# Graph attention and graph convolution, two layers: hub steps one y block later, and the pair with block 0 ninth of ten

## The chip, the cores and the metric

The kernel runs on one core of a Trainium2 chip. The core has five engines with instruction queues of their own: TensorE (PE in the profile; its weight loads are PEld), VectorE (DVE), ScalarE (ACT), GpSimd (POOL) and SyncE (SP), which here only issues transfers. The metric is device time in microseconds, the median of several runs.

## The reference

There are 2708 rows (nodes) of 1024 features, all float32, and a 0/1 adjacency matrix `adj` of 2708 x 2708 with few ones a row; early rows have more than late ones.

```python
# layer 0
q, k, v = x @ W_q.T + b_q, x @ W_k.T + b_k, x @ W_v.T + b_v
z = (q @ k.T) / sqrt(1024) * adj
z = where(z == 0, -10000, z)
x = layernorm(x + relu(softmax(z, axis=1) @ v))
# layer 1
x = layernorm(x + adj @ (x @ weight) + bias)
```

Because the masked scores vanish in the softmax, only the scores on a row's own neighbours matter. A row without neighbours gets the mean over all rows.

## The kernel before, in words

The kernel does not form the 2708 x 2708 score matrix. It finds each row's neighbour list, gathers the neighbours' rows of `x` by indirect transfers, and works on those. `(x @ W_q.T) @ (x @ W_k.T).T` is rewritten as `y @ x.T` with `y = x @ M`, where `M` is the product of the two weight matrices; `adj @ (x @ W)` is computed as `(adj @ x) @ W`. If a list is longer than the kernel has room for, a flag is raised and a dense version runs instead; with these inputs it does not.

**Blocks.** The rows are sorted by number of neighbours in two families and cut into 22 blocks of up to 128 rows. `SLOTS` says how many neighbour slots a block has: 15, 11, 8, 6, 5, 4, 3, 2 for blocks 0 to 7, then 13, 5, 4, 4, 3, 3, 3, 2, 2, 2, 1, 1, 0, 0. A gather of one slot is one POOL instruction: one row of 4 KB for each of 128 partitions. The 32 rows with the most neighbours are the *hub*. Their neighbours are dealt out in shares of 11 slots over 128 partitions (`tab_h`, `valid_h`, `part`); block 0 with 15 slots holds the rest of its rows and shares. When block 0 is transposed for the matmuls ("flipped"), `flip_shares` (L840 to L852) adds the hub's shares `part` and block 0's `r` together with one-hot matrices `to_h` and `to_0`. So block 0's flip needs both the hub's sums and block 0's own.

**Stages.** First come the weights' product `M` (L709) and the neighbour lists (`list_columns`, L235 to L245, on DVE). Then there is the loop over the first family's y blocks, `for b in range(FAMILY)`, b from 0 to 7. In it, `y_block(b)` issues 16 matmuls (L378; two records each in the profile), evicts each half on DVE (L320), has SP load a later block of `x` (L297) and stores y (L369). `row_constants` (L746) makes one dot product a row on DVE. `sort_begin(1)` and `sort_end(1)` sort the second family; `sort_end` has two matmuls, L632 and L634. `next(deal)` runs one step of the hub's dealing, the generator `deal_hub`. Its steps are:

- step zero, POOL gathers of the hub rows' adjacency;
- step one, a search for the up to 80 neighbours in each quarter row on DVE (L503 and L505), the count `n_q` (L508), and a store of the keys (POOL, L514);
- step two, matmul L519 of `n_q` over the four quarters and the sizes of the shares on DVE (L521 to L528);
- step three, matmuls L531 and L532, DVE work on places and positions (L534 to L567, with `to_h` last), and a POOL gather of the hub's records;
- step four, transpose L570 and the masks `far_h` and `far_0`;
- step five, eleven small POOL gathers (`found`, L435);
- step six, the tables `valid_h`, `tab_h` and `less_h`.

Steps five and six are issued in the next loop, at the second family's first and fifth block. L519, L531/L532 and the sort's L632 all write the tile `mm`, of which there is one buffer.

Then the second family's y blocks run with attention among them: an attention job gathers y (`yg`, L435), which needs the stores of the first eight y blocks, and the neighbours' x (`g`, L441, nine buffers), scores them (L917) and sums (L974, L1058). Then pairs of blocks are projected with `W_v`, normalised and scattered to `x1`.

**Layer 1** (L1290 to L1390) works the blocks in ten pairs, `units`, which are numbered from 0 here. For each `units[i]`, `sum_rows` gathers and sums the neighbours' rows of `x1` (POOL L441, DVE L1307 and L1310), `turn1` flips the two sums (PE L836, or L849 for block 0) and makes sums and differences of their halves (DVE L1097 to L1100), `gather_x1` brings the residual `xr` (ScalarE L1320 copies the bias, and a POOL gather at L435 adds the rows to it), and `work1` does seven products of half matrices in place of eight (`pair_products`, matmuls at L306; evictions at L320 and L1347). `finish1` normalises and scatters to `out` (POOL L823). In iteration i the order is: finish `units[i-1]`, flip `units[i+1]` and gather its residuals, gather and sum `units[i+3]`, then the products of `units[i]`. The blocks 20 and 21, which have no neighbours, are finished behind `units[4]` and `units[6]`.

**Order.** A planner fixes the order of every engine's queue when the kernel is built. It goes by priority, which is the order in which the code issues instructions (evictions are marked more urgent), and by when it believes inputs to be ready. On the chip each queue runs in that order, and an instruction whose input is late holds up what is behind it.

Of the kernel before, what the change touches and what calls it, by code (L numbers as in the profile page):

```python
# [80 lines left out]
def sparse_part(ctx, tc, x, xT, adj, wqT, wkT, wvT, bq, bk, bv, w1, b1, out):  # L81
# [29 lines left out]
    with es:  # L111
# [69 lines left out]
        def bcast_rows(dst, col):  # L181

            for g in range(DC // 4):
                tr = p_tr.tile([P, 4, P], F32, name="tr")
                for k in range(4):
                    c = g * 4 + k
                    nc.tensor.transpose(tr[:, k, :], col[:, c:c + 1].to_broadcast([P, P]), ident)
                nc.scalar.copy(dst[:, g * HALF:(g + 1) * HALF], tr.rearrange("p a b -> p (a b)"))
# [37 lines left out]
        def list_columns():  # L226
            b = listed[0]
            listed[0] += 1
            n, a = rows[b], loaded[b]

            nc.scalar.activation(junk[:n], a[:n], AF.Sign, accum_out=cnt[:n, b:b + 1])  # L231
            nc.scalar.activation(junk[:n], a[:n], AF.Relu, scale=-1.0, accum_out=neg[:n, b:b + 1])
            at = lists.tile([P, RANGES, 8], U16, name="at_a", bufs=2)
            for i in range(RANGES):
                nc.vector.max_index(at[:n, i], ones[:n, :8], a[:n, cuts[i] + 8 * i:cuts[i + 1] + 8 * i + 8])  # L235
            there = lists.tile([P, RANGES, 8], F32, name="there", bufs=2)
            nc.vector.tensor_tensor(there[:n], at[:n], ends[:n], op=ALU.is_lt)
            few = lists.tile([P, 8 * RANGES], F32, name="few", bufs=2)
            few3 = few.rearrange("p (i k) -> p i k", k=8)
            nc.vector.tensor_tensor(few3[:n], at[:n], base[:n], op=ALU.add)  # L240
            nc.vector.tensor_tensor(few3[:n], few3[:n], there[:n], op=ALU.mult)
            for i in range(0, KEYS, 8):
                nc.vector.max(keys[:n, b, i:i + 8], few[:n])
                if i + 8 < KEYS:
                    nc.vector.match_replace(few[:n], keys[:n, b, i:i + 8], few[:n], 0.0)  # L245
            load_adj()
# [115 lines left out]
        def load_last():  # L362
            r0, n = (NB - 1) * P, rows[-1]
            nc.sync.dma_start(out=x_last[:, :, :n], in_=xT[:, r0:r0 + n].rearrange("(c p) n -> p c n", p=P))
# [6 lines left out]
        def y_block(b):  # L371
            yo = yos[b % 3]
            to, base = halves_of(yo), halves_of(y_bc)
            firsts = []
            for h in range(NH):
                po = bank()
                for c in range(DC):
                    put = nc.tensor.matmul(po, xts[b][:, c, :], m_q[c // 4][h][:, c % 4], start=(c == 0), stop=(c == DC - 1))  # L378
                    if c % (DC // 2) == 0:
                        firsts.append(put)  # L380
                add(to[h], po, base[h])
            products.append(put)
            if b != NB - 2:
                column_sums(b, firsts)
            load_x()
            y_store(b, yo)
# [41 lines left out]
        def follow(later, earlier, same=False):  # L428

            kind = mybir.DependencyClass.NoSync if same else mybir.DependencyClass.Sync  # L430
            tc.add_manual_dep(later.ins, earlier.ins.name, mybir.DependencyInfo(kind, mybir.DependencyReason.DATA),
                              reason="an engine's queue shall not stand still for a transfer")
# [168 lines left out]
        def quarters_of(name):  # L601
            return [[wv_pool.tile([P, DC // 2, HALF], F32, name=f"{name}{i}{j}", tag=f"v{2 * i + j}") for j in range(2)]
                    for i in range(2)]
# [82 lines left out]
        def records_back(f, behind=None):  # L686
            b0, nb = families[f]
            bs, js = slice(b0, b0 + nb), slice(0, max(SLOTS[max(b0, 1):b0 + nb]))
            if f == 0:

                deg0 = lists.tile([P, 1], F32, name="deg0")
                follow(nc.vector.tensor_copy(deg0, tab0[:, DEG:DEG + 1]), products[-1])
                nc.vector.tensor_scalar_add(deg0[:HUB], deg0[:HUB], float(-J0))
                masks(valid0, less0, deg0)
            put = nc.vector.tensor_copy(degs[:, bs], tabs[:, bs, DEG])
            follow(put, products[-1] if behind is None else behind, same=behind is not None)
            masks(valid[:, bs, js], less[:, bs, js], degs[:, bs])
# [37 lines left out]
        def load_rows_of_c():  # L735
            a = la.tile([P, AW], F32, name="a")
            for k in range(2):
                b = c_blocks.pop(0)
                load_rows(a[:, k * D:(k + 1) * D], x, b * P, rows[b])
                c_ready.append((b, a[:, k * D:(k + 1) * D]))  # L740

        def row_constants(count):
            for _ in range(count):
                b, xg = c_ready.pop(0)
                n = rows[b]
                nc.vector.scalar_tensor_tensor(junkc[:n], xg[:n], 1.0, u_bc[:n], op0=ALU.mult, op1=ALU.mult,  # L746
                                               accum_out=c_all[:n, b, 0:1])
                if b in (FAMILY - 1, NB - 1):
                    f = int(b >= FAMILY)
                    b0, end = families[f][0], sum(families[f])  # L750
                    nc.vector.tensor_scalar(c_all[:, b0:end, 0], c_all[:, b0:end, 0], y_bc[:, D:D + 1], None, op0=ALU.add)
                    full = min(end, NB - 1)
                    nc.sync.dma_start(out=y_ds[f][:(full - b0) * P, D:].rearrange("(b p) e -> p b e", p=P), in_=c_all[:, b0:full])
                    if full < end:
                        nc.sync.dma_start(out=y_ds[f][(full - b0) * P:, D:], in_=c_all[:rows[full], full])

        for b in range(FAMILY):
            while done < min(NB, EARLY + 2 * (b + 1)):
                list_columns()
                done += 1  # L760
            y_block(b)
            if b == 1:
                bcast_rows(u_bc, u_col)
            if b == 2:
                load_last()
            if b in (0, 1, 3, 4, 5):
                next(deal)
            row_constants(len(c_ready))
            for _ in range({3: 3, 4: 3, 5: 2, 6: 3}.get(b, 0)):
                load_rows_of_c()  # L770
            if b == FAMILY - DC // 2 - 3:
                wv_q = quarters_of("wv")
            elif FAMILY - DC // 2 - 2 <= b < FAMILY - 2:
                for c in range(2 * (b - FAMILY + DC // 2 + 2), 2 * (b - FAMILY + DC // 2 + 2) + 2):
                    for h in range(NH):
                        put = nc.sync.dma_start(out=wv_q[c // 4][h][:, c % 4, :],
                                                in_=wvT[c * P:(c + 1) * P, h * HALF:(h + 1) * HALF])
                        follow(put, products[-2])
            if b == FAMILY - 4:
                sort_begin(1)  # L780
            if b == FAMILY - 3:
                later_records = sort_end(1)
            if b == 0:
                records_back(0)
# [502 lines left out]
        bias1 = hp.tile([P, D], F32, name="bias1", tag="bias")  # L1287
        nc.sync.dma_start(out=bias1, in_=b1.to_broadcast([P, D]))

        units = [(19, 18), (17, 16), (15, 1), (14, 2), (7, 8), (9, 3), (4, 10), (6, 0), (5, 11), (12, 13)]  # L1290
        assert sorted(last + [b for unit in units for b in unit]) == list(range(NB))
        last_norm = applied[-1]
        firsts = []
# [73 lines left out]
        for i, unit in enumerate(units):  # L1367
            for p in pending:
                finish1(*p)
            if i + 1 < len(units):  # L1370
                turned1[i + 1] = turn1(units[i + 1], got1.pop(i + 1))
                xrs[i + 1] = [gather_x1(b, k) for k, b in enumerate(units[i + 1])]
            if i == 0:
                got1[2] = [sum_rows(b, k, halves_turned[-1]) for k, b in enumerate(units[2])]
            if i + 3 < len(units):
                got1[i + 3] = [sum_rows(b, k) for k, b in enumerate(units[i + 3])]
            if i == 3:
                sum_rows("hub")
            pending = list(zip(unit, *work1(unit, *turned1.pop(i), xrs.pop(i))))
            if i in (4, 6):  # L1380
                b = last[i // 2 - 2]
                pending.append((b, gather_x1(b), None))
# [319 lines left out]
```

## Time and profile before

| | |
|---|---|
| runs, us | 1075.88, 1076.21, 1081.52; median 1076.21 |
| the profiled execution's own time | 1077.36 us |
| its span, first to last instruction | 1075.6 us |
| busy: PE, DVE, POOL, ACT | 981.1, 821.1, 472.9, 432.8 us |
| mean granted TensorE clock | 0.961 of full speed |
| first family's y blocks on PE | about 139 to 269 us |
| layer 1 on PE | 760.6 to about 1058 us |

The profile is one execution. A line of a timeline gives the start and the length in microseconds, the engine, the line of the kernel, the operation and its tiles, and in brackets how long the engine stood idle before it and what ended that. The list of waits adds such idle times up: engine, line, what it waited for, total, times, longest. The granted clock of PE is a share of full speed.

### The profile page before, as it was taken

To read this page: it belongs to the slowest core of one execution; us is meant where nothing else is said; L and a number is where in the kernel's file an instruction comes from. 1 tells how busy PE (TensorE), PEld (TensorE's weight loads), DVE (VectorE), ACT (ScalarE), POOL (GpSimd) and SP (SyncE) were. 2 spreads that over 40 slices of the span, in tenths; PEclk is the share of its full clock that TensorE was granted. 3 is DMA by queue.
4 is the path that set the end of the run, shared out by engine and by line. 5 is a ranking of instruction groups with operands and counts; after the bars stand their busy time and mean duration, and the time that the engine had idled before them with its cause. 6 is when DMAs were issued, how large, how long until landed. Compare 5 with 4: busy or idle time off the path is not lost.

```text
span 1075.6 us, 10690 instructions
## 1 busy us (share of the span) xinstructions
PE 981.1 (91%) x2761; PEld 464.8 (43%) x2761; DVE 821.1 (76%) x2039; ACT 432.8 (40%) x902; POOL 472.9 (44%) x520
## 2 busy tenths in 40 slices
PE   8999999598999998889999999997699899769993
PEld 6444444243444443345454444443344344334441
DVE  8999698980588987997999999544668879667332
ACT  4599896042223322332433443323222432244421
POOL 0000500025267665343665663211778678867300
PEclk9999999799999998999999999999799999979997
DMA  9698858968587767545456875226778698888601
GB/s 356 186 294 242 254 161 280 317 211 233 153 274 242 232 220 219 155 143 170 142 175 216 290 237 187 82 75 236 191 284 240 177 323 320 261 227 290 135 39 42
DMA packets 105782, 228.80 MB, mean 213 GB/s; under 512 B 22500, under 2 KB 49900, under 8 KB 105710
## 3 DMA queue, kind: packets, MB, share of 16 engines
q0 software_dynamic: 48192, 147.52, 43.8%
q1 hardware_dynamic: 57518, 80.50, 23.8%
q8 instruction: 23, 0.38, 0.1%
q14 instruction: 49, 0.40, 0.1%
HBM read 217.60 MB, written 33.68 MB: 234 GB/s over the span
## 4 chain that ended last, share of the span: by engine, by line
PE 30%; DVE 18%; issue 16%; DMA 10%; POOL 8%; ACT 1%; SPq 0%; POOLq 0%; DVEq 0%; ACTq 0%
PE po L306 24%; POOL g L441 5%; PE po L378 4%; DVE junkv L917 3%; DVE r L1310 3%; DMA g<-in_x_dram,tabs 2%; DVE r L974 2%; DMA g<-x_d,tabs 2%; DMA g<-x_d,tab_h 2%; PE tr L836 1%; DVE yo L320 1%; DVE r L1058 1%; POOL yg L435 1%; POOL xr L435 1%; DMA out_dram<-t,tabs 1%
## 5 line engine op out<-in xcount | busy, mean ns | idle before, releaser
L378 PE MATMUL po<-m,xt 128*128 128x512 f32 x672 | 297.3, 603 | 8.3 <-DVE yo L320 4.8
L378 PEld LDWEIGHTS po<-m,xt 128*128 128x128 f32 x672 | 129.4, 194 | 171.7 <-issue 163.3
L306 PE MATMUL po<-t,s_all 128*128 128x512 f32 x320 | 146.5, 601 | 9.8 <-DVE xr L320 8.4
L917 DVE SCALAR_TENSOR_TENSOR junkv<-yg,g 128x1024 uint8<-128x1024 f32 x108 | 131.7, 1220 | 26.6 <-DMA g<-in_x_dram,tabs 11.9
L441 POOL DMA_INDIRECT g<-in_x_dram,tabs x84 | 108.0, 1286 | 57.2 <-DVE r L974 16.7
L1310 DVE SCALAR_TENSOR_TENSOR r<-g,valid,r 128x1024 f32<-128x1024 f32 x77 | 98.2, 1282 | 20.9 <-DMA g<-x_d,tabs 10.2
L709 PE MATMUL po<-wk_o,wq_o 128*128 128x512 f32 x256 | 110.5, 592 | 0.0
L306 PEld LDWEIGHTS po<-t,s_all 128*128 128x128 f32 x320 | 60.6, 192 | 90.6 <-issue 71.2
L441 POOL DMA_INDIRECT g<-x_d,tabs x66 | 77.8, 1179 | 25.1 <-issue 16.5
L424 ACT ACTIVATE junka<-xt 128x128 f32<-128x128 f32 x168 | 51.7, 308 | 78.9 <-PE po L378 61.7
L235 DVE FIND_INDEX8 at_a<-ones,a 128x8 uint16<-128x83 f32 (+3 forms) x132 | 82.7, 630 | 0.0
L879 ACT ACTIVATE junks<-t,lnm 128x1024 uint8<-128x1024 f32 (+1 forms) x40 | 45.9, 1148 | 89.7 <-DVE lnm L877 89.4
L974 DVE SCALAR_TENSOR_TENSOR r<-g,pr,r 128x1024 f32<-128x1024 f32 x64 | 81.7, 1280 | 0.2
L306 PE MATMUL po<-wv,s_all 128*128 128x512 f32 x160 | 74.5, 610 | 4.0 <-DVE s_all L1097 4.0
L837 ACT COPY rT<-tr 128x512 f32<-128x512 f32 x76 | 41.0, 590 | 91.2 <-PE tr L836 89.3
L709 PEld LDWEIGHTS po<-wk_o,wq_o 128*128 128x128 f32 x256 | 48.3, 190 | 59.3 <-issue 58.6
L306 PE MATMUL po<-t,rT 128*128 128x512 f32 x160 | 73.7, 603 | 0.3 <-DVE t L320 0.3
L306 PE MATMUL po<-w,rT 128*128 128x512 f32 x160 | 72.8, 600 | 0.0
L306 PE MATMUL po<-w,s_all 128*128 128x512 f32 x160 | 72.1, 592 | 0.0
L306 PE MATMUL po<-wv,rT 128*128 128x512 f32 x160 | 70.5, 592 | 0.0
L892 ACT ACTIVATE t<-t,nmr,rstd 128x1024 f32<-128x1024 f32 (+1 forms) x40 | 49.1, 1237 | 41.7 <-DVE nmr L891 33.5
L231 ACT ACTIVATE junk<-a 128x2756 uint8<-128x2756 f32 (+1 forms) x22 | 55.0, 2500 | 9.5 <-DMA a<-in_adj_dram 4.2
(354 smaller groups left out, 1393.9 us busy)
## 6 DMA issues: line engine op xcount, KB each, us to landing
xt<-in_xT_dram SPq DMA_DIRECT2D x21, 512.0 KB
y_d<-yo SPq DMA_DIRECT2D x21, 512.0 KB
a<-in_x_dram SPq DMA_DIRECT2D x21, 512.0 KB
a<-in_adj_dram SPq DMA_DIRECT2D x21, 413.5 KB
a<-in_adj_dram SPq DMA_DIRECT2D x21, 338.5 KB
a<-in_adj_dram SPq DMA_DIRECT2D x21, 263.5 KB
wq_i<-in_wqT_dram SPq DMA_DIRECT2D x8, 512.0 KB
wk_i<-in_wkT_dram SPq DMA_DIRECT2D x8, 512.0 KB
```

Source lines behind the costliest of these rows:

```text
L231: nc.scalar.activation(junk[:n], a[:n], AF.Sign, accum_out=cnt[:n, b:b + 1])
L235: nc.vector.max_index(at[:n, i], ones[:n, :8], a[:n, cuts[i] + 8 * i:cuts[i + 1] + 8 * i + 8])
L306: put = nc.tensor.matmul(acc, a[:, k], w[:, k], start=start and k == 0, stop=stop and k == DC // 2 - 1, skip_group_check=True)
L378: put = nc.tensor.matmul(po, xts[b][:, c, :], m_q[c // 4][h][:, c % 4], start=(c == 0), stop=(c == DC - 1))
L424: put = nc.scalar.activation(junka[:, :xt.shape[2]], xt[:, c, :], AF.Copy, accum_out=xs[:, c, b:b + 1])
L441: nc.gpsimd.indirect_dma_start(out=dst[:n], out_offset=None, in_=src, in_offset=bass.IndirectOffsetOnAxis(ap=at, axis=0), bounds_check=N - ...
L709: nc.tensor.matmul(po, wq_o[i // 2][:, o, i % 2 * P:(i % 2 + 1) * P], wk_o[:, o, hs], start=(o == 0), stop=(o == DC - 1))
L879: nc.scalar.activation(junks[:n], t[:n], AF.Square, bias=nm[:n], accum_out=vs[:n])
L892: applied.append(nc.scalar.activation(t[:n], t[:n], AF.Identity, bias=nmr[:n], scale=rstd[:n]))
L917: nc.vector.scalar_tensor_tensor(junkv[:n], yg[:n, :D], scale, xg[:n], op0=ALU.mult, op1=ALU.mult, accum_out=s)
L974: nc.vector.scalar_tensor_tensor(r[:n], xg[j][:n], pr[:n, j:j + 1], r[:n], op0=ALU.mult, op1=ALU.add)
L1310: put = nc.vector.scalar_tensor_tensor(r[:n], xg[:n], ok[:n, j:j + 1], r[:n], op0=ALU.mult, op1=ALU.add)
```

## The change

Two edits.

In the loop over the first family's y blocks, steps zero and one of the hub's dealing stay behind blocks 0 and 1; steps two, three and four are issued behind blocks 4, 5 and 6 instead of 3, 4 and 5. Steps five and six stay where they are.

In layer 1, `units[7]` and `units[8]` change places, so (5, 11) comes eighth and (6, 0), the pair with block 0, ninth of ten. The hub's gathers and sums are issued in iteration 4, behind those of `units[7]`, instead of in iteration 3 behind those of `units[6]`. Block 0's pair has its own sums issued in iteration 5 instead of 4. No instruction is added or removed.

```diff
@@ -763,7 +763,7 @@
             if b == 2:
                 load_last()
-            if b in (0, 1, 3, 4, 5):
+            if b in (0, 1, 4, 5, 6):
                 next(deal)
             row_constants(len(c_ready))
@@ -1287,7 +1287,7 @@
-        units = [(19, 18), (17, 16), (15, 1), (14, 2), (7, 8), (9, 3), (4, 10), (6, 0), (5, 11), (12, 13)]
+        units = [(19, 18), (17, 16), (15, 1), (14, 2), (7, 8), (9, 3), (4, 10), (5, 11), (6, 0), (12, 13)]
@@ -1374,7 +1374,7 @@
                 got1[i + 3] = [sum_rows(b, k) for k, b in enumerate(units[i + 3])]
-            if i == 3:
+            if i == 4:
                 sum_rows("hub")
             pending = list(zip(unit, *work1(unit, *turned1.pop(i), xrs.pop(i))))
```

## The prediction

> **What bounds the kernel now.** The page comes first: 1075.6 us of span, TensorE (PE) busy for 91% of it. So time lies either in PE's instructions or in the 9% where PE stands still, and a reordering can only touch the latter. The list of waits, whole span, gives the long ones (total us, times, longest):
>
> ```profile
> POOL keys_d L514 <- DVE junk_h L523: 59.9, 1, 59.9
> ...
> POOL found L435 <- DVE to_h L567: 19.6, 1, 19.6
> ...
> PE tr L849 <- DVE r L1310: 15.8, 1, 15.8
> ...
> PE tr L836 <- DVE r L1307: 13.9, 1, 13.9
> ...
> PE mm L519 <- DVE junk_h L508: 12.5, 1, 12.5
> ```
>
> Three PE waits exceed 6 us. L836 is the entry into layer 1, which the change leaves alone; L519 (the hub's step two in y) and L849 (block 0's flip in layer 1) are what its two edits move. Next, PE's timeline (start, length, instruction, idle before it) around L519:
>
> ```profile
> 194.82 3.60 PE L378 MATMUL po<-m,xt 128*128 128x512 f32 x8
> 210.87 0.58 PE L519 MATMUL mm<-n_q,alike 128*128 128x1 f32 x2 [12.46 <-DVE junk_h L508]
> 211.32 11.39 PE L378 MATMUL po<-m,xt 128*128 128x512 f32 x20
> 222.55 0.38 PE L531 MATMUL mm<-lower,more 128*128 128x128 f32 x2
> ```
>
> A y block is 32 records of about 0.43 us (8 records take 3.44). The wait stops block 4 with 20 of its records undone; and those 20 take 11.39 us instead of 8.6. The stretch table says why: granted clock 0.50 from 210.8 to 216, 1.00 from 217. So the wait costs 12.46 + 2.8 = 15.3 us. VectorE (DVE) is busy without a gap from 176 to 211, so L508 can't be had sooner.
>
> The same around L849, and what DVE and GpSimd (POOL) do there:
>
> ```profile
> 907.66 7.03 PE L306 MATMUL po<-w,rT 128*128 128x512 f32 x16
> ...
> 935.26 0.30 PE L849 MATMUL tr<-to_h,part 128*128 128x32 f32 x2
> 951.41 0.74 PE L849 MATMUL tr<-to,r 128*128 128x96 f32 x2 [15.85 <-DVE r L1310]
> ...
> 981.50 2.16 PE L836 MATMUL tr<-ident,r 128*128 128x128 f32 x16
> 983.49 7.03 PE L306 MATMUL po<-w,rT 128*128 128x512 f32 x16
> ```
> ```profile
> 939.51 11.85 DVE L1310 SCALAR_TENSOR_TENSOR r<-g,valid,r 128x1024 f32<-128x1024 f32 x9
> ```
> ```profile
> 891.52 1.50 POOL L441 DMA_INDIRECT g<-x_d,tab_h x1 [0.30 <-issue]
> ...
> 917.94 1.03 POOL L441 DMA_INDIRECT r<-x_d,tabs x1 [0.30 <-issue]
> ...
> 943.35 0.99 POOL L441 DMA_INDIRECT g<-x_d,tab x1 [0.30 <-issue]
> ```
>
> PE asks at 935.4 for block 0's sum; DVE finishes it at 951.4; POOL, which issues the gathers in order, has been full since 855 and ends block 0's at 944.3. Clock 0.50 again from 951.4 to 957: 2.8 us more.
>
> **Edit A, hub steps in y.** Nothing is added or removed. Steps two to four (5 small DVE operations and matmul L519; matmuls L531 and L532, some 35 DVE operations of 0.08 to 0.35 us, one POOL gather; transpose L570 and 9 DVE operations) come one y block later. No SP transfer belongs to them. The schedule is written by the planner in priority order, so I take L519 to fall where block 4 ends, 20 records on: PE works 198.4 to 207.0 in place of waiting. L508 stays in DVE's full queue; one more 0.6 us eviction may now precede it, so 211.5. Remaining wait 4.5 us. What a wait of that size costs in clock: the 4.35 us wait at 841.2 stretches its eight records from 3.60 to 5.35 (1.75 us), the 3.98 us wait at 481.2 to 6.17 (2.6); I take 2.2. Gain 15.3 - 4.5 - 2.2 = 8.6 us.
>
> The Trainium skill ("TensorE: Matmul & The Clock Gate", Part 1: The HAM clock gate) puts both the idle window that halves the clock and the warm-up at about 3.4 us. That speaks against the edit, because a wait cut to 4.5 us is still long enough to throttle; by that rule each cold start loses 1.7 us, and the sum would be 12.46 - 4.5 = 8.0 us. This trace shows 5.6 us at half clock after the long waits.
>
> What the steps move past: at the end of block 5, L531/L532 now stand beside the sort's matmuls L632/L634, with which they share the one `mm` bank; L632 has to wait until L534 and L536 have read it. Before, those came 0.8 us after L532, behind one eviction. Bounds 0 to 2 us; hidden if the planner puts block 6's matmuls between; I take 0, since they are ready. L570's transpose comes 14 us after L531 as before, and its `row` is done 10 us after it: hidden.
>
> On POOL, the 12 small gathers after `to_h` start at 232.4 now. L531 moves from 222.55 to about 228 (211.6 + 13.7 + 2.2), so `to_h` to 238, or 242 if the sort's 3.4 us of DVE work and an eviction get ahead. Twelve gathers at 1.25 us and ten at 1.29 follow: POOL is free at 266 to 270. The first yg gather, at 277.93 now (17.77 us of idle before it), needs y's block 7 stored; 8.6 us earlier is 269.3. Cover remains by 3 us at one end and is short by 1 at the other. If the small gathers came 8.6 us later still, the whole gain would be gone, since attention starts with yg: edit A's lower bound is 0, its upper one 15 (no wait left). From there on everything hangs on yg, y stores and DVE, and all move together.
>
> **Edit B, layer 1's order.** Again the same instructions. units[7] becomes (5, 11) with 8 gathered rows a partition, units[8] (6, 0) with 18; the hub's 11 come after units[7]'s instead of before. The flip at PE's 935 then needs 8 instead of 29 rows behind 891.5. POOL's rows: the hub's 11 take 891.5 to 909.0 (1.59 each), two scatters and two residual gathers to 917.6 (8.3), block 6 and 0's 18 to 944.3 (26.4, 1.47 each). The new order has the four first (8.3, and 3.3 of waiting, since ScalarE normalises the scattered rows until 894.8), then 8 x 1.46 = 11.7: done at 915, summed some 3 us later. The wait at 935 is gone. So is the 1.99 us wait on xr at 928, because the residual gathers run 14 us sooner.
>
> Now units[8]'s flip is late next. PE: units[5] starts at 907.66; seven products of 3.43 end at 931.7, the flip 1.8, units[6] to 957.5. POOL from 915: hub 17.5, five others (blocks 20's, two scatters, two residuals, 2.1 each) 10.4, the 18 26.4: 969. The last gather's landing and its sum, about 2: 971. PE waits 13.5 us there. The 32 flip records take 4.6 us at half clock, and 1 us more is lost in what follows: units[7]'s products start as if at 976.6, against 983.5 now. Gain 6.9, say 7.
>
> Bounds: all 37 gathers at the 1.30 us pace of 940 to 943 and the nine others at 1.6 give 957, summed at 960: PE waits 3, gain near 20. DVE lagging POOL by the 7 us it lags today gives 976, gain 2. I take 971 because it uses the rows of these very gathers, and because DVE has no hub work left then. Units 7 to 9 follow on PE as now; the last pair's six gathers are issued by about 985 for a flip near 1001, so hidden. ScalarE's copies for xr ride on PE's pace; SP has nothing here.
>
> **Sum.** 8.6 + 7 = 15.6. The profiled execution took 1077.36 us, 1.15 above the runs' median 1076.21: 1077.4 - 15.6 = 1061.8, and 1060.6 as a median. Forecast 1061.
>
> **Rivals.** *Only A pays* (1068 = 1076.2 - 8.6): the order on PE is fixed, and before, L849 stands ahead of a product of units[5]. If block 0's flip again gets ahead of two of units[6]'s products, PE starts those 6.9 us late, which is edit B's gain. For it: that row. Against: it got ahead where units[5] waited for late xr gathers, and those come earlier now.
>
> *Only B pays* (1069 = 1076.2 - 7): the small gathers hold POOL until 278, and attention starts no sooner. For it: the 19.6 us POOL wait on `to_h` is the same queue. Against: 17.8 us of POOL idle before yg.
>
> *Slower* (1085): the planner puts block 0's flip ahead of all seven products of units[6]. They then start at 976.6, and end 24.0 later at 1000.6, 17.1 behind 983.5; A gives back 8.6; net +8.5. It decides from 4.5 products on ((6.9 + 8.6) / 3.43). For it: the planner does believe the sums ready long before they are. Against: the flip is issued after units[6]'s products, and passed one of seven last time.
>
> *It doesn't do what it says* (1076): the planner holds L519 and the flip where PE asks for them now. Against: their priorities follow program order.
>
> **How the numbers follow.** Chances: forecast 0.54, with an own range of 1049 to 1068 (A 5 to 12, B 2 to 15); only A 0.14; only B 0.10; nothing moves 0.08; slower 0.14. About 0.5%, 5.4 us, is what a measurement can tell from no change: below 1070.8 is faster, above 1081.6 slower. Faster takes the first case whole and most of the next two: 0.75; same 0.11; slower 0.14. The range 1048 to 1077 leaves out the slower case and a few in a hundred at the fast end.
>
> **What would show it.** A: PE's wait at L519 near 4.5 us, behind a whole block 4; yg near 269. B: no L849 wait near 935, one of 3 to 18 us near 958 on units[8]. Wrong if L519's wait stays above 10, if yg stays at 278, if `mm` makes L632 wait, or if L849 stands among units[6]'s products.

## The result and the profile after

The changed kernel took 1073.15 us (median) beside 1076.76 for the kernel before: ratio 0.9963, 95% interval 0.9943 to 0.9984, so some 4 us faster, less than the 0.5% that the prediction took as its bound. 1061 was forecast. Two later measurements of the same kernel, on two chips, each beside the kernel before, gave 0.9954 (0.9924 to 0.9984) and 0.9939 (0.9908 to 0.9971). The profiled execution took 1075.25 us, its span 1073.5.

The list of waits of the changed kernel, whole span (total us, times, longest):

```profile
POOL keys_d L514 <- DVE keys_h L513: 58.7, 1, 58.7
...
PE po L378 <- DVE yo L320: 17.7, 7, 6.3
...
PE tr L836 <- DVE r L1307: 13.9, 1, 13.9
...
POOL rec_h L435 <- DVE to_h L567: 13.2, 1, 13.2
...
PE mm L519 <- DVE junk_h L508: 4.7, 1, 4.7
...
PE mm L632 <- DVE bad L536: 3.1, 1, 3.1
```

Both long waits that the change was about are shorter or gone: L519 fell from 12.5 to 4.7 us, and L849's 15.8 us is no longer listed. One line is new, L632's wait for the hub's L536, and one has grown: TensorE waits 17.7 us for evictions of y (4.8 before). TensorE's timeline around the hub's steps:

```profile
192.46 15.18 PE L378 MATMUL po<-m,xt 128*128 128x512 f32 x35
212.32 0.59 PE L519 MATMUL mm<-n_q,alike 128*128 128x1 f32 x2 [4.68 <-DVE junk_h L508]
212.77 16.32 PE L378 MATMUL po<-m,xt 128*128 128x512 f32 x32
...
234.75 1.25 PE L632 MATMUL mm<-hot,lower 128*128 128x266 f32 x2 [3.06 <-DVE bad L536]
235.80 13.26 PE L378 MATMUL po<-m,xt 128*128 128x512 f32 x28
```

Block 4 stands whole in front of L519, as forecast. But L632 then waits for the one `mm` bank, and the clock falls a second time (the stretch table grants 0.51 from 235 to 238 us). VectorE's timeline shows why the bank was held:

```profile
231.34 1.22 DVE L746 SCALAR_TENSOR_TENSOR junkc<-a,u_bc 128x1024 uint8<-128x1024 f32 x1 [5.27 <-DMA a<-in_x_dram]
...
233.76 0.67 DVE L320 TENSOR_TENSOR yo<-po,y_bc 128x512 f32<-128x512 f32 x1
234.37 0.27 DVE L534 COPY place<-mm 128x128 f32<-128x128 f32 x1
234.56 0.14 DVE L536 TENSOR_SCALAR bad<-mm 128x1 f32<-128x1 f32 x1
```

L534 and L536, which empty the bank, stand behind a row constant that waits 5.27 us for rows of `x`; before, they stood ahead of it. GpSimd's timeline in the same stretch:

```profile
243.54 0.98 POOL L435 DMA_INDIRECT rec_h<-tab_d,row_i  x1 [13.24 <-DVE to_h L567]
...
257.32 0.94 POOL L435 DMA_INDIRECT found<-keys_d,at_i  x1 [0.30 <-issue]
258.57 1.01 POOL L441 DMA_INDIRECT g<-in_x_dram,tabs  x1 [0.30 <-issue]
...
268.96 0.95 POOL L435 DMA_INDIRECT xr<-in_x_dram,tabs  x1 [0.30 <-issue]
281.43 0.95 POOL L435 DMA_INDIRECT yg<-y_d,tabs  x1 [11.51 <-issue]
```

`to_h` is done 11 us later than before, the twelve small gathers follow it, and the large `g` gathers come behind them, eight of the nine from 258.6 to 268.7. (The ninth went ahead alone at 229.) GpSimd is free at 269.9, inside the forecast's 266 to 270, and yet yg starts at 281.43 instead of 269.3; before, it was 277.93. So attention starts 3.5 us later, not 8.6 earlier. (The 277.93 holds a loss of its own, of some 5 us, which the section on the stop in the evictions shows.) Layer 1, TensorE, around block 0's flip:

```profile
942.64 1.13 PE L306 MATMUL po<-w,rT 128*128 128x512 f32 x2 [3.07 <-DVE t L1347]
...
954.15 5.40 PE L306 MATMUL po<-t,s_all 128*128 128x512 f32 x8 [3.52 <-DVE xr L320]
...
973.13 0.31 PE L849 MATMUL tr<-to_h,part 128*128 128x32 f32 x2
...
985.60 0.36 PE L849 MATMUL tr<-to,r 128*128 128x96 f32 x2
...
1012.90 5.33 PE L306 MATMUL po<-t,s_all 128*128 128x512 f32 x8 [3.17 <-DVE xr L320]
```

The flip waits for nothing now: the planner laid its pieces between products of `units[7]`. Three waits of 3 us on evictions stand in its place, 9.8 us together. Layer 0's last matmul (L1278) came 8.5 us later than before (754.99 against 746.45), and from there to the last product it took 300.8 us instead of 311.3. Read like this, edit A lost 8.5 us and edit B won 10.5. The experiments were to test that.

### The profile page after: what moved, and what is told of

Its sections match the earlier page's. It is cut to its first block, busy times and chain, and to the rows that moved or that the text cites. A ratio compares the mean times of both kernels' runs of the same rounds, so it can differ in the third digit from the quotient of the medians.

```text
span 1073.5 us, 10686 instructions
## 1 busy us (share of the span) xinstructions
PE 984.4 (92%) x2761; PEld 463.1 (43%) x2761; DVE 818.2 (76%) x2039; ACT 431.7 (40%) x902; POOL 473.8 (44%) x520
## 4 chain that ended last, share of the span: by engine, by line
PE 28%; DVE 16%; issue 16%; DMA 13%; POOL 10%; ACT 2%; SPq 1%; POOLq 0%; DVEq 0%; ACTq 0%
PE po L306 17%; PE po L378 8%; POOL g L441 5%; DVE junkv L917 3%; DMA g<-in_x_dram,tabs 3%; DMA g<-x_d,tabs 2%; POOL xr L435 2%; DVE r L974 2%; DMA xr<-x_d,tabs 2%; DMA a<-in_x_dram 1%; DVE yo L320 1%; DVE r L1058 1%; PE tr L836 1%; POOL out_dram L823 1%; POOL r L441 1%
## 5 line engine op out<-in xcount | busy, mean ns | idle before, releaser
L378 PE MATMUL po<-m,xt 128*128 128x512 f32 x672 | 299.3, 605 | 17.8 <-DVE yo L320 17.7
L378 PEld LDWEIGHTS po<-m,xt 128*128 128x128 f32 x672 | 129.3, 195 | 183.5 <-issue 155.3
L306 PE MATMUL po<-t,s_all 128*128 128x512 f32 x320 | 151.2, 617 | 13.0 <-DVE xr L320 6.9
L917 DVE SCALAR_TENSOR_TENSOR junkv<-yg,g 128x1024 uint8<-128x1024 f32 x108 | 131.6, 1219 | 40.3 <-DMA g<-in_x_dram,tabs 15.5
L441 POOL DMA_INDIRECT g<-in_x_dram,tabs x84 | 111.3, 1325 | 72.6 <-DVE r L974 16.8
```

What stands on the lines that cost most here:

```text
L306: put = nc.tensor.matmul(acc, a[:, k], w[:, k], start=start and k == 0, stop=stop and k == DC // 2 - 1, skip_group_check=True)
L441: nc.gpsimd.indirect_dma_start(out=dst[:n], out_offset=None, in_=src, in_offset=bass.IndirectOffsetOnAxis(ap=at, axis=0), bounds_check=N - ...
L917: nc.vector.scalar_tensor_tensor(junkv[:n], yg[:n, :D], scale, xg[:n], op0=ALU.mult, op1=ALU.mult, accum_out=s)
```

## The experiments

Ratios are to the kernel before on the same chip. In the tables that follow the runs, yg is the start of the first yg gather and "last y" the start of the last L378 record, each from one profile.

**Edit A alone, edit B alone.** First the hub's dealing is edited and layer 1 is not, then the other way round.

```diff
-            if b in (0, 1, 3, 4, 5):
+            if b in (0, 1, 4, 5, 6):
```

> Edit A alone: the hub's steps two to four behind blocks 4, 5 and 6; layer 1 as before. Theory: in the changed kernel's trace TensorE reaches its 393rd y record 8.0 us sooner than before (321.2 against 329.2), but the attention chain of VectorE and GpSimd starts 3.6 us later (285.9 against 282.3), and layer 0 ends 8.5 us later (754.99 against 746.45). If that shift belongs to edit A, this kernel takes about 1076.5 + 8.5 = 1085 us (1081 to 1089), with yg near 281 and the flip of the attention's pairs near 477. Rival: edit A is worth next to nothing, the later end of layer 0 being made up for in layer 1, and edit B brings the 4 us: then 1075 to 1079. Forecast's own theory, A pays 8.6: 1068.

Measured: 1077.86 us beside 1074.76; ratio 1.0021 (0.9994 to 1.0048).

```diff
-        units = [(19, 18), (17, 16), (15, 1), (14, 2), (7, 8), (9, 3), (4, 10), (6, 0), (5, 11), (12, 13)]
+        units = [(19, 18), (17, 16), (15, 1), (14, 2), (7, 8), (9, 3), (4, 10), (5, 11), (6, 0), (12, 13)]
...
-            if i == 3:
+            if i == 4:
```

> Edit B alone: units[7] and units[8] change places and the hub's sums come one unit later; the hub's dealing as before. Theory: from the end of layer 0 to the last product the changed kernel takes 300.8 us against 311.3, so edit B is worth about 10 us and this kernel 1066 us (1063 to 1069). Rival: B brings only the 3 to 4 us that the whole change brings, 1072 to 1074. The wait of 15.85 us at L849 is gone in both; the theory has no wait over 5 us in its place.

Measured: 1064.86 us; ratio 0.9893 (0.9852 to 0.9935), that is 11.5 us.

B does what the theory said, and its ratio is lower than the whole change's 0.9963, measured apart; the intervals do not overlap. A alone brings nothing and rather costs: 8.6 us of gain, the forecast's term, is outside its interval. The theory's 8.5 us of loss is outside too; 2 us is the middle. The two profiles differ up to layer 1 only by edit A, and both evict y evenly:

| | A alone | B alone |
|---|---|---|
| TensorE at y record 225, us | 247.1 | 250.5 |
| yg, us | 276.72 | 272.86 |
| last y, us | 469.4 | 464.7 |

With A, TensorE leads by 3.4 us before block 7, and still yg comes 3.9 us later and the y blocks end 4.7 us later. That the lead is worth nothing unless yg comes earlier is what the rest is about.

**The `mm` bank.** On edit A alone, the sort's first matmul writes a tile of the other pool:

```diff
-            before = p_mm.tile([P, HALF], F32, name="mm")
+            before = p_tr.tile([P, 4, P], F32, name="tr").rearrange("p a b -> p (a b)")
```

> Edit A alone, with the sort's first matmul (L632) writing a tile of the p_tr pool instead of the one mm bank. Nothing else is edited. Theory: L632 no longer waits (3.06 us in the changed kernel) and the clock does not fall there, so TensorE leads by some 4 us more in the y blocks (about 12 us at the 393rd record); but the attention chain still starts with yg near 281, so the time stays with edit A alone, within 2 us: 1083 to 1087. Rival: the bank clash is what eats edit A's gain: then yg comes some 4 us sooner and the time is 4 us or more below edit A alone.

Measured: 1072.41 us; ratio 0.9970 (0.9944 to 0.9996), 5.5 us below edit A alone. The wait at L632 is gone, and TensorE is at y record 225 at 241.5 instead of 247.1: the clash cost 5.6 us, 3 of it waiting, the rest put down to clock and order. The theory's time fell: yg did come sooner, at 268.26, since the store of block 7 was issued at 256.18, just before the large gathers began at 256.59. The rival was right.

**The small gathers behind the large ones.** On edit A alone, step five is issued two blocks later and takes the hub's records with it (step six one block later), so that the planner puts the nine `g` gathers first:

```diff
@@ deal_hub
-            row_i = small("row_i", 1, I32)
+            row_i = const.tile([P, 1], I32, name="row_i")
...
-            gather_at(tab_ds[0][:, :], row_i, P, rec_h)
...
             for j in range(HUB_SLOTS):
                 gather_at(keys_d[:, :], at_i[:, j:j + 1], P, found[:, j:j + 1])
+            gather_at(tab_ds[0][:, :], row_i, P, rec_h)
...
-                if b in (FAMILY, FAMILY + 4):
+                if b in (FAMILY + 2, FAMILY + 5):
```

> Edit A alone, with step five of the dealing issued two blocks later and the gather of the hub's records moved from step three into step five; step six one block later. On GpSimd's queue the nine g gathers then stand ahead of the twelve small gathers instead of behind them. Theory: the nine gathers run from about 229 to 241 instead of 258 to 270; the evictions that stopped until the end of that burst (273.1 in the changed kernel) stop earlier, y's block 7 is stored as soon as TensorE has done it (about 263), and yg is issued near 271 to 274; attention starts 8 us sooner than with edit A alone, and the time is 6 to 10 us below it: 1075 to 1079. Rival: yg is late for another reason (the twelve small gathers, or block 7 itself), and yg and the time stay as with edit A alone: yg 279 to 282, 1083 to 1087.

Measured: 1068.64 us; ratio 0.9948 (0.9921 to 0.9975), 9.2 us below edit A alone by the medians, 7.8 by the ratios. GpSimd's timeline of this kernel:

```profile
235.91 0.99 POOL L441 DMA_INDIRECT g<-in_x_dram,tabs  x1 [0.30 <-issue]
241.92 0.96 POOL L435 DMA_INDIRECT found<-keys_d,at_i  x1 [5.01 <-DVE to_h L566]
...
268.05 0.94 POOL L435 DMA_INDIRECT yg<-y_d,tabs  x1 [10.14 <-issue]
```

The store of block 7 is issued at 262.10 here and at 261.78 in edit A alone, the same moment; yg follows 6.0 us later here and 14.9 us later there. Evictions did not stop in this profile of edit A alone, so the reason given in the expectation was not the one at work between these two. The transfers show what was. From the store's issue to yg, first edit A alone (262 to 276 us), then this kernel (262 to 268 us); the rows are queue, packets, MB and share of the 16 engines, then issues with their number and KB each, for the gathers the median time to landing in us:

```profile
q0 software_dynamic: 996, 3.42, 62.5%
q1 hardware_dynamic: 1216, 1.07, 24.4%
...
y_d<-yo SPq DMA_DIRECT2D x1, 512.0 KB
xt<-in_xT_dram SPq DMA_DIRECT2D x1, 512.0 KB
g<-in_x_dram,tabs POOLq DMA_INDIRECT x4, 10.5
```
```profile
q1 hardware_dynamic: 1184, 1.05, 61.4%
...
y_d<-yo SPq DMA_DIRECT2D x1, 512.0 KB
```

SP's queue moves about the same in both, 1.07 and 1.05 MB, a load of `x` and the store; alone they need 6 us, beside 3.4 MB of gathers 14.9. In the two profiles with only L632 in the other pool, the burst runs beside this store too, and yg follows it by 12.1 us (edit A alone) and 17.7 us (the changed kernel, below). The Trainium skill ("DMA: Bandwidth & Descriptors", Issuing engines are not separate DMA queues) says that transfers started by ScalarE, SyncE and GpSimd run on the same 16 DMA engines and interleave; these rows agree, with 62.5% and 24.4% of the engines' time for the two queues.

**The same two mends on the changed kernel.** The changed kernel, and it with the first diff above (L632), with the second (small gathers last) and with both, on one chip:

> The changed kernel once more, unedited. Two questions. First, in its earlier profile VectorE's evictions stood still until 273.1 us, while in edit A alone, whose order is the same up to layer 1, they did not (241 to 268, one every 6.9 us). If that stop was one execution's disturbance, it is gone here and yg comes near 277 as in edit A alone, behind a store of y's block 7 that takes some 15 us because the nine g gathers run beside it; if it belongs to the kernel, it is here again, with yg near 281. Second, whether the two edits add up: edit A alone 1.0021, edit B alone 0.9893, product 0.9914, which is 1065.5 us for 1074.8 before. Rival: part of B's gain is lost when A is there, and the ratio stays near the 0.9963 measured, 1070 to 1072.

> The changed kernel with the sort's matmul L632 writing a p_tr tile instead of the one mm bank. With edit A alone this took 5.5 us off (1077.86 to 1072.41). Theory (the bank clash and its cold clock stand in the y blocks before yg, so they cost attention's start): 4 to 7 us below the changed kernel of this call. Rival: with edit B there the gain does not reach the end: within 2 us of it.

> The changed kernel with the twelve small gathers (step five and the hub's records) behind the nine g gathers; the bank clash stays. With edit A alone this took 9.2 us off (1077.86 to 1068.64). Theory (the nine gathers beside block 7's store are what delays yg): yg near 268 and 7 to 11 us below the changed kernel of this call. Rival: the gain needed the old layer 1 to show: within 3 us of it.

> Both mends on the changed kernel: L632 in a p_tr tile, and the twelve small gathers behind the nine g gathers. The first brings block 7 some 5.5 us earlier, the second frees its store. Theory: yg near 262, no wait of TensorE between L519 (2.5 to 3 us) and the entry to the pairs, except for evictions among the attention's work; about 1052 to 1058 us, the fastest of all. Rival: once yg is free of both, attention is held by something else (the first y stores, DVE's evictions), and the second mend adds less than 3 us to the better of the two alone.

| kernel | us | ratio to before | yg, us | last y, us |
|---|---|---|---|---|
| changed, again | 1073.70 | 0.9954 (0.9924 to 0.9984) | 279.73 | 472.8 |
| L632 in the other pool | 1066.73 | 0.9897 (0.9865 to 0.9928) | 276.93 | 470.5 |
| small gathers last | 1057.53 | 0.9823 (0.9784 to 0.9861) | 267.96 | 455.9 |
| both | 1054.90 | 0.9794 (0.9760 to 0.9828) | 262.24 | 453.0 |

The changed kernel itself stayed near its first 0.9963, as that expectation's rival had it, and its evictions stopped again. The kernel with both mends is the fastest of all, 22 us below the kernel before by the ratio. Its TensorE timeline has the hub's steps and the sort without a wait after L519, and yg starts where the forecast's working would have it, and earlier:

```profile
209.68 0.38 PE L519 MATMUL mm<-n_q,alike 128*128 128x1 f32 x2 [2.83 <-DVE junk_h L508]
...
225.80 0.69 PE L632 MATMUL tr<-hot,lower 128*128 128x266 f32 x2
```
```profile
254.50 0.94 POOL L435 DMA_INDIRECT rec_h<-tab_d,row_i  x1 [0.30 <-issue]
255.74 0.94 POOL L435 DMA_INDIRECT xr<-in_x_dram,tabs  x1 [0.30 <-issue]
262.24 0.94 POOL L435 DMA_INDIRECT yg<-y_d,tabs  x1 [5.56 <-DVE yo L320]
```

The first mend gave 6.2 us, as its theory had it. The second gave 14.1 us, more than the 7 to 11 expected: yg came 11.8 us sooner, and TensorE's waits for evictions among the attention's work fell from 13.1 to 3.3 us, which the theory did not foresee and no run takes apart. Both together gave 3.1 us more than the second alone, with overlapping intervals, so the expectation's rival (less than 3 us more) can't be excluded.

**Both parts and a control on one more chip.** The last kernel is edit B with the old dealing and both mends, so the three diffs above without edit A's:

> Edit A alone once more, now on the same chip as edit B alone and the changed kernel. In its first profile evictions ran on during the nine g gathers (one every 6.9 us, yg 276.7); in the changed kernel's two profiles they stood still until 272 to 273 (yg 279.7 and 281.4). If that stop hangs on edit B, which lies 500 us later, it is absent here and present in the changed kernel beside it; if it hangs on the chip or on chance, kernels with and without B fall alike or at random. Time: theory (edit A costs 2 to 5 us in layer 0 through the later burst and the bank clash, and part of it is made good): 1.000 to 1.005 of before. Rival (the first measurement flattered it; A costs the 6 us missing between B's gain and the whole change's): 1.005 to 1.010.

> Edit B alone once more, on that same chip. Theory: B is worth 10 to 11 us wherever it runs: 0.987 to 0.992 of before. Rival: the first 0.9893 was high by chance and B is worth what the whole change is, 0.994 to 0.997.

> The changed kernel, unedited, beside its two parts on one chip. Theory: its ratio is that of edit A alone times that of edit B alone, within 0.004, and near the 0.9963 and 0.9954 measured. Rival: it is more than 0.004 above that product, so the two edits hinder each other.

> Control: edit B with the old dealing (no edit A) and both mends, L632 in a p_tr tile and step five two blocks later with the hub's records in it. With the old dealing L632 does not wait and the small gathers stay ahead of the nine g gathers, which end before block 7 is stored. Theory: the mends have nothing to mend; the time is edit B alone's, within 3 us, and the 10 us by which the changed kernel with both mends beats edit B alone (0.9794 against 0.9893) belong to edit A unhindered. Rival: the mends carry the gain by themselves, and this kernel is 6 us or more below edit B alone.

| kernel | us | ratio to before | yg, us | last y, us |
|---|---|---|---|---|
| A alone | 1083.60 | 1.0039 (1.0019 to 1.0059) | 279.93 | 469.6 |
| B alone | 1070.01 | 0.9911 (0.9881 to 0.9942) | 273.58 | 467.2 |
| changed | 1073.30 | 0.9939 (0.9908 to 0.9971) | 278.68 | 471.0 |
| B with both mends | 1067.17 | 0.9892 (0.9864 to 0.9921) | 273.12 | 463.7 |

All four theories held. A costs 4.2 us of 1079 here (2.3 the first time), B is worth 9.6 (11.5), and their product, 0.9950, is the changed kernel's 0.9939 within the error. On the first pair's chip the product was 0.9914, against 0.9954 on another for the changed kernel; the intervals overlap.

The control is 0.0019 from B alone, inside both intervals: without edit A there is nothing to mend. Against it, the changed kernel with both mends is 0.0098 lower, and their intervals, taken on two chips, do not overlap. That is about 10.5 us for edit A when neither the bank nor the burst of gathers is in its way.

**The stop in the evictions.** The expectations ask of VectorE's evictions stopping during the burst of large gathers. The stop is in all three profiles of the changed kernel, in the second ones of edit A alone and of edit B alone, and in the kernel before's own, so it belongs to neither edit. VectorE's evictions, changed kernel first, then edit A alone in its first profile, then B alone in its second, then the kernel before, with its first yg gather:

```profile
256.08 0.69 DVE L320 TENSOR_TENSOR yo<-po,y_bc 128x512 f32<-128x512 f32 x1 [5.77 <-issue]
273.10 1.29 DVE L320 TENSOR_TENSOR yo<-po,y_bc 128x512 f32<-128x512 f32 x2 [16.33 <-remote]
```
```profile
254.19 0.69 DVE L320 TENSOR_TENSOR yo<-po,y_bc 128x512 f32<-128x512 f32 x1 [5.77 <-PE po L378]
261.06 0.69 DVE L320 TENSOR_TENSOR yo<-po,y_bc 128x512 f32<-128x512 f32 x1 [6.17 <-PE po L378]
267.93 0.69 DVE L320 TENSOR_TENSOR yo<-po,y_bc 128x512 f32<-128x512 f32 x1 [6.17 <-PE po L378]
```
```profile
262.68 1.29 DVE L320 TENSOR_TENSOR yo<-po,y_bc 128x512 f32<-128x512 f32 x2 [18.41 <-PE po L378]
265.38 0.69 DVE L320 TENSOR_TENSOR yo<-po,y_bc 128x512 f32<-128x512 f32 x1 [1.41 <-PE po L378]
```
```profile
253.74 0.69 DVE L320 TENSOR_TENSOR yo<-po,y_bc 128x512 f32<-128x512 f32 x1 [12.73 <-PE po L378]
263.71 1.29 DVE L320 TENSOR_TENSOR yo<-po,y_bc 128x512 f32<-128x512 f32 x2 [9.28 <-remote]
```
```profile
277.93 0.94 POOL L435 DMA_INDIRECT yg<-y_d,tabs  x1 [17.77 <-issue]
```

Eight profiles have it in all, and in seven of them it ends with the burst of large gathers. With the old dealing that is at 263, before block 7's second half is due, and yg moves by only 0.7 us between B alone's two profiles (272.86 and 273.58). With edit A the burst lasts until 273, over block 7's second half, and yg moves by 3.2 us (276.72 and 279.93). In the changed kernel it is the stop itself that delays yg:

```profile
273.82 0.43 SPq L369 DMA_DIRECT2D y_d<-yo  x1
```

TensorE's records end block 7 at 262.8, but its store is issued at 273.82, when the burst is over, and yg follows 7.6 us later; in the kernel's two other profiles 7.0 and 6.8. So two things make the burst costly beside block 7's store: where evictions go on, the store itself takes 14.9 us; where they stop, it is issued some 10 us late.

The profile of the kernel before, from which the forecast was worked out, lost time by the stop as well. Behind it TensorE paused three times and ran at half clock from 264.3 to 267.7, so that block 7 took it 19.4 us instead of the 13.7 of edit B alone, whose hub steps and y blocks are those of the kernel before. Its yg of 277.93 is 4 to 5 us later than in the three other profiles with the old dealing (272.9 to 273.6). Against those, the changed kernel's yg is not 3.5 but 5.1 to 8.6 us late.

## Why the prediction was wrong

**The bound and edit A's gain on TensorE: right.** L519's wait is 4.68 us where 4.5 was said, 1.4 to 3.5 in the nine other profiles with edit A. Half clock behind it cost 2.3 us where 2.2 was said (block 5's 32 records took 16.32 us, as many before 13.98). With the bank clash removed (edit A with L632 in the other pool), TensorE passes y record 225 at 241.5, with edit B alone, which has the old dealing, at 250.5: 9.0 us of lead for the 8.6 forecast.

**"I take 0, since they are ready": wrong.** The bank clash was bounded at 0 to 2 us and cost 5.6. The price was taken from where L534 and L536 stood before, behind one eviction; at their new place VectorE's queue holds the row constants as well, whose rows of `x` landed only at 231.3. That was the failure named as "`mm` makes L632 wait".

**"8.6 us earlier is 269.3": the step that decided.** GpSimd's queue was worked out well: `to_h` 243.2 for 238 to 242, free at 269.9 for 266 to 270. The step then took GpSimd's issue time for the whole claim of the gathers. Edit A moves them from ahead of block 7's store to beside it. In edit A alone's first profile their 3.4 MB on the same DMA engines turn the store's 6 us into 14.9; in the changed kernel's profiles the evictions stop until the burst is over, and the store is issued some 10 us late. Yg at 279 to 281 in place of 269.3 gave up the term. Moving the large gathers ahead of the small ones and so of the store, with edit A kept, gave it back: shown by the runs with that edit, and by the control without A. That the burst beside the store is the cause is shown by them; why evictions stop beside it is not. The starting point, 277.93, was also high by 4 to 5 us, which one profile could not tell: 8.6 us ahead of the three others is 264 to 265, and with both mends yg came at 262.24.

**"From there on everything hangs on yg": right, and against the forecast.** In the changed kernel TensorE reaches y record 393 at 321.2 us, 8.0 sooner than before, and then loses all of it in the 17.7 us of waiting for evictions, which stand in VectorE's queue among attention's work. That the 8.0 is so near the forecast's 8.6 is luck: 5.6 of it is what the kernel before's profile lost in block 7, and edit B alone reaches that record at 322.6. The late start of 3.6 us (VectorE's first L917 at 285.93 against 282.27) grows to 8.4 by the last y eviction (479.1 against 470.8); against edit B alone it is 8.6 from the start (277.28) and 10.7 at the last eviction (468.4). GpSimd's queue also came out in another order there; what part that has, no run isolates.

**Edit B: the wait that goes was right, the one that comes was not, and the size was too small.** 7 was forecast, 9.6 and 11.5 measured, inside the term's 2 to 20. The wait of 13.5 us at `units[8]`'s flip did not come. The step assumed the flip ahead of `units[7]`'s products; the planner put it between them, so that TensorE had those to do while the sums, complete at 985, were late. What was lost instead is the three waits of 3 us, in place of L849's 15.8 and the 2.0 at 928.

**The rivals.** "Only B pays" (1069) names the right half of the change and comes nearest to what happened; its price for A was 0 and its reason (small gathers hold GpSimd until 278) was not the one, for GpSimd was free by 270. "Only A pays" had it the wrong way round. The slower case did not occur: in the changed kernel's profile the flip does not stand ahead of `units[6]`'s products. The sum of 15.6 should have read: B about 10.5, A minus 2 to minus 4 (below its stated bound of 0), thus 6 to 8, of which 4 to 6.6 was measured.

## What to carry to other kernels

A lead that one engine wins before a hand-over counts only if the hand-over itself comes earlier: follow the chain to the first instruction of the next stage and price its last transfer at the moment where it will run, with what else will be moving then. Take the starting time of that hand-over from more than one profile. When steps are moved past each other, an instruction's queue time and its data's time on the DMA engines are two claims, and both have to be laid against the critical store. A bank shared by two steps is only free once the reader has run, and the reader's place is set by everything queued ahead of it at its new position.

## What the hardware showed that was not expected

In eight of the fourteen profiles, the kernel before's among them, VectorE's evictions of y stopped about the burst of 512 KB indirect gathers: VectorE, waiting for TensorE's matmuls of y, stood idle for 9 to 19 us where 6 are usual between two evictions. In seven of the eight it went on within 2 us of the last of the burst's data. In the eighth, the changed kernel with only L632 in the other pool, there are two shorter stops, until 258.5 and 271.3 us, and the data run until 276. In the kernel before TensorE's records end the first half block that was evicted late at 244.8, four us ahead of the first large gather, so that the burst need not be the whole cause. In the changed kernel the records show TensorE starting matmuls without a gap all the while (249 to 325 us); in the kernel before it paused three times, 3.4 us together. In the changed kernel ScalarE's wait for L378 was 12.45 us, VectorE's 16.33, and SP's load of `x` came at 273.13. All four profiles taken on one chip were free of it, among them two with the order of queues that has it elsewhere. So were the two of the changed kernel with the small gathers last, on a chip where the kernel without that edit had it. The one instruction-fetch packet of that stretch comes after the stop ends in seven of the eight (274.1 us in the changed kernel) and so doesn't explain it. What stops the evictions stays open.
